# Gathers, first sums and norms at the end of a decoder layer's experts, put in another order

## The chip, the cores and the metric

The kernel runs on one core of one Trainium2 chip. What counts is the time of one execution on the device, in microseconds (us). A core has five engines, each with an instruction queue of its own that it works off in order: TensorE (PE in the profile; PEld is its loading of weights), VectorE (DVE), ScalarE (ACT), GpSimd (POOL) and SyncE (SP), which here only issues transfers. Engines wait for one another through semaphores.

## The reference

One decoder layer over 16 x 256 tokens of 256 values: an attention, a cross attention and a mixture of four experts, each added to the stream and followed by a layer norm without gain. The change touches only the end of the third part:

```python
logits = jnp.einsum('bsh,he->bse', x, router_w) + router_b + load_balancer
rw, sel = jax.lax.top_k(logits, K)           # K = 2 of 4 experts
rw = jax.nn.softmax(rw, axis=-1)
...
gathered = jnp.take_along_axis(stack, sel[..., None], axis=2)
return (rw[..., None] * gathered).sum(axis=2)
...
x = _layernorm(x + _L0_ffn_ref(x, ...), axis=-1)   # (x - m) / sqrt(v + eps)
```

So each token's result is x plus two weighted expert rows, normed over its 256 values.

## The kernel before

The 4096 tokens are 32 rows of 128 (`xs`, one SBUF tile of 128 x 32 x 256 float32) and go in 8 pairs of 4 rows (`CPB` = 4). Pairs 0 to 6 are group 0, pair 7 (`last`) is group 1. While the attention still ran, each token was written by indirect DMA into a list of each expert it chose, one DRAM tensor `xlist[g]` per group; `moe["place"]` holds the token's two places there and `moe["weight"]` its two weights. The place of index 0 is always that of the expert with the lower number.

Each expert works through its list in blocks of 512 rows: `load` fetches a block (SP), `turn` transposes it on TensorE and copies the result with ScalarE and VectorE into a buffer of the ring xeT, the products run, ScalarE applies Gelu, Silu or Relu, and `result` adds the bias on VectorE into the one buffer `ye` and has SP store it over the block's rows in the list. A block of at most 256 rows takes a shorter form; how many rows a list has is known only at run time, so each block stands in `tc.If` branches (`block`, L499 and L502), which every engine passes for itself. The products' PSUM banks are eight, taken in turn (`bank`).

`rest` runs the last stage. Expert 1 of group 0 (`second`) is done first, then experts 2 and 0 together in a loop, then expert 3 (`fourth`) in four blocks, with the three parts of expert 2 of group 1 (`third(1, 0)`, a generator) put between them. `beyond(3, 4, n, fourth)` holds three nested levels for further blocks of expert 3 (L713); with these inputs they are skipped. Then follow experts 0, 1 and 3 of group 1: `first(1, 0)`, `second(1, 0)`, `fourth(1, 0)`.

The results come back by `gather`: four indirect DMAs of GpSimd per pair and choice, from the list into a slot (L671). Slots are the two halves of `ya`, `x3` and, late, the four quarters of a second hidden buffer `hb`. Choice 0 of group 0 needs experts 0 to 2 only, so it is gathered between the blocks of `fourth(0, ..)`, two pairs at a time, and added on VectorE behind each block (`adds`, L682, one instruction per row, `x + t * weight`). Choice 1 of all seven pairs is gathered behind the last of these blocks, 28 transfers in a row. `sums(n)` adds the second choice of n pairs with L682, which also yields each row's sum, and scales these to minus the mean (L691). `end` squares on ScalarE (L701, with a sum per row), takes the inverse root on VectorE (L702, `rsqrt` at L158 to L165, L704), scales the rows on ScalarE (L706) and has SP store each pair (L708). Sums and ends come as 2, 2, 3 and 1 pairs, the first sums ahead of `second(1, 0)`, its end behind it, and so on.

In this stage every engine keeps the order in which the code is written; only in straight code between branches do the engines overlap freely. A gather waits for all earlier stores into its list, and a store into a list for all earlier gathers from it.

Of the kernel before, what the change touches and what calls it, by code (L numbers as in the profile page):

```python
# [20 lines left out]
NPAIR = B // 2  # L21
TB = 2 * S
CPB = TB // P
# [80 lines left out]
def decoder_kernel(ctx: ExitStack, tc: tile.TileContext, a: dict, out: bass.AP):  # L104
    nc = tc.nc
    PE, DVE, ACT, POOL, SP = nc.tensor, nc.vector, nc.scalar, nc.gpsimd, nc.sync
# [3 lines left out]
    out_v = out.flatten_outer_dims().rearrange("(n p) d -> p n d", p=P)  # L110
# [43 lines left out]
    def rsqrt(pool, v, n, E=DVE):  # L154


        yi = pool.tile([P, n], I32, tag=f"rs_y{n}", name="rs_y")
        E.tensor_scalar(yi, v.bitcast(I32), -0.5, float(0x5F3759DF), ALU.mult, ALU.add)  # L158
        y = yi.bitcast(F32)
        t = pool.tile([P, n], F32, tag=f"rs_t{n}", name="rs_t")  # L160
        for _ in range(3):
            if E is DVE:
                E.scalar_tensor_tensor(t, y, -0.5, y, ALU.mult, ALU.mult)  # L163
                E.tensor_tensor(t, t, v, ALU.mult)  # L164
                E.scalar_tensor_tensor(y, t, 1.5, y, ALU.add, ALU.mult)  # L165
# [178 lines left out]
    def group(q):  # L344
        return int(q >= GROUPS[1][0])
# [116 lines left out]
    class Experts:  # L462
# [17 lines left out]
        def next(self, name):  # L480
            t = self.rings[name].pop(0)
            self.rings[name].append(t)
            return t
# [180 lines left out]
            self.loaded += [self.load(0, 2, 0), self.load(0, 0, 0)]  # L664


        def gather(self, q, k):
            t = self.slots.pop(0)
            self.slots.append(t)
            for n in range(CPB):  # L670
                POOL.indirect_dma_start(  # L671
                    t[:, n, :], None, xlist[group(q)][:],
                    bass.IndirectOffsetOnAxis(ap=moe["place"][:, q * CPB + n, k:k + 1], axis=0),
                )
            self.gathered.append((q, k, t))

        def add(self, sums=None):
            q, k, t = self.gathered.pop(0)
            for n in range(CPB):
                x = xs[:, q * CPB + n, :]  # L680
                kw = {} if sums is None else {"accum_out": sums[:, n:n + 1]}
                DVE.scalar_tensor_tensor(  # L682
                    x, t[:, n, :], moe["weight"][:, q * CPB + n, k:k + 1], x, ALU.mult, ALU.add, **kw
                )
            return q, t

        def sums(self, n):

            m = self.fl.tile([P, 3 * CPB], F32, tag="means", name="means", bufs=2)
            done = [self.add(m[:, k * CPB:(k + 1) * CPB]) for k in range(n)]  # L690
            DVE.tensor_scalar(m[:, :n * CPB], m[:, :n * CPB], -1.0 / D, None, ALU.mult)  # L691
            return m, done

        def end(self, m, done):

            w = len(done) * CPB
            m = m[:, :w]
            v = self.fl.tile([P, 3 * CPB], F32, tag="vars", name="vars", bufs=2)[:, :w]
            rows = [(q * CPB + n, t[:, n, :]) for q, t in done for n in range(CPB)]
            for i, (r, t) in enumerate(rows):  # L700
                ACT.activation(t, xs[:, r, :], AF.Square, bias=m[:, i:i + 1], accum_out=v[:, i:i + 1])  # L701
            DVE.tensor_scalar(v, v, 1.0 / D, EPS, ALU.mult, ALU.add)  # L702
            y = rsqrt(self.fl, v, w)
            DVE.tensor_tensor(m, m, y, ALU.mult)  # L704
            for i, (r, t) in enumerate(rows):
                ACT.activation(xs[:, r, :], xs[:, r, :], AF.Identity, bias=m[:, i:i + 1], scale=y[:, i:i + 1])  # L706
            for q, t in done:
                SP.dma_start(out=out_v[:, q * CPB:(q + 1) * CPB, :], in_=xs[:, q * CPB:(q + 1) * CPB, :])  # L708

        def beyond(self, e, i0, i1, work):  # L710

# [8 lines left out]
        def rest(self, fl, xw, xb, rb):  # L720
            self.fl, self.xw, self.xb, self.rb = fl, xw, xb, rb
            self.ring(fl, "hid", 2, [P, 8, TB])
            self.ring(fl, "h2", 1, [P, CPB, D])
            self.ring(fl, "h2T", 1, [P, 2, TB])
            n = SIZES[0] // (4 * P)
            t5 = self.turn(self.loaded.pop(0))
            self.second(0, 4, self.ready.pop(0))
            b_ = self.turn(self.loaded.pop(0))
            self.second(0, 5, t5)
            self.beyond(1, 6, n, self.second)  # L730
            self.known(1)


            ya = self.wb.tile([P, 2, CPB, D], F32, tag="cxp", name="ya")
            self.slots, self.gathered = [ya[:, 0], ya[:, 1]], []
            a_, x0, x1 = self.loaded.pop(0), self.load(0, 3, 0, self.x3), self.load(0, 3, 1, ya[:, 1])
            assert not self.loaded and not self.ready
            with ExitStack() as levels:
                for i in range(n):
                    levels.enter_context(tc.If(self.count[0][4] > 4 * P * i))  # L740
                    a_ = self.turn(a_)
                    b = self.third(0, i, b_)
                    next(b)
                    if i + 1 < n:
                        b_, a1 = self.load(0, 2, i + 1), self.load(0, 0, i + 1)
                    c = self.first(0, i, a_)
                    next(c)
                    next(b)
                    if i + 1 < n:
                        b_, a_ = self.turn(b_), a1  # L750
                    next(c)
                    next(b)

            pairs = iter(range(NPAIR - 1))

            def gathers(k, most=2):
                for _ in range(most):
                    q = next(pairs, None)  # L760
                    if q is not None:
                        self.gather(q, k)

            def adds():
                while self.gathered:
                    self.add()

            x2, y2, x3 = self.load(0, 3, 2), self.load(1, 2, 0), self.load(0, 3, 3)
            ta, tb = self.rings["xeT"]
            self.turn(x0, ta)  # L770
            self.turn(x1, tb)
            gathers(0)
            self.fourth(0, 0, ta)
            adds()
            gathers(0)
            b = self.third(1, 0, self.turn(y2, ta))
            next(b)
            self.turn(x2, ta)
            y0, y1 = self.load(1, 0, 0), self.load(1, 1, 0)
            self.fourth(0, 1, tb)  # L780
            adds()
            gathers(0)
            next(b)
            self.turn(x3, tb)
            y3 = self.load(1, 3, 0)
            self.fourth(0, 2, ta)
            adds()
            gathers(0)
            next(b)
            self.turn(y0, ta)  # L790
            self.fourth(0, 3, tb)
            adds()
            self.rings["xeT"] = [tb]
            self.beyond(3, 4, n, self.fourth)


            ha, hb = self.rings["hid"]
            self.rings["hid"] = [ha]
            hb = hb.rearrange("p f t -> p (f t)").rearrange("p (s c d) -> p s c d", s=4, d=D)
            self.slots += [self.x3] + [hb[:, k] for k in range(4)]  # L800
            last = NPAIR - 1
            pairs = iter(range(last))
            gathers(1, last)
            copies = (DVE.tensor_copy, DVE.tensor_copy)
            c = self.first(1, 0, ta)
            next(c)
            self.turn(y1, tb, copies=copies)
            next(c)
            self.turn(y3, ta, copies=copies)
            part = self.sums(2)  # L810
            self.second(1, 0, tb)
            self.end(*part)
            part = self.sums(2)
            self.gather(last, 0)
            self.fourth(1, 0, ta)
            self.gather(last, 1)
            self.end(*part)
            self.end(*self.sums(3))
            self.add()
            self.end(*self.sums(1))  # L820
            assert not self.gathered

    experts = Experts

# [875 lines left out]
```

## Time and profile before

| | us |
|---|---|
| median of 8 runs | 1749.22 (1746.13 to 1751.86) |
| the profiled execution | 1748.03 |
| its span in the profile | 1746.3 |
| PE busy | 1634.1 (94%) |
| DVE, ACT, POOL busy | 918.2, 969.7, 537.2 |

A line of a timeline or a chain gives the start in us from the span's begin, the time in us, engine, source line, operation and output<-inputs by the program's names, how many, and in brackets how long the engine sat idle before and what ended that. The stages of the end, from the timeline of PE:

| stage | us |
|---|---|
| fourth(0, 0) | from 1515.67 |
| fourth(0, 1) | from 1552.44 |
| fourth(0, 2) | from 1591.62 |
| fourth(0, 3) | from 1626.85 |
| first(1, 0) | from 1656.99 |
| second(1, 0) | from 1681.22 |
| fourth(1, 0) | from 1695.00 |
| last matmul's result read (L546) | 1712.49 |
| last store issued (L708) | 1741.82 |

### The profile page before, as it was taken

The numbers are of one execution on the slowest core, as the hardware profiler recorded it, in microseconds if no ns is written. First come the engines' busy times: TensorE is split into PE (matmuls) and PEld (weight loads), VectorE is DVE, ScalarE is ACT, GpSimd is POOL, SyncE is SP. The second block draws the span as 40 slices with busy tenths as digits, with TensorE's granted clock in tenths as the row PEclk, the third lists the DMA queues.
The fourth block names the chain that finished last, engine by engine and source line by source line (L and its number), as shares of the span: only waits on it lengthen the run. The fifth ranks groups of instructions, "written<-read, shape, count | busy, mean of one in ns | idle before, by whom it ended". The sixth has DMA issues, their size and how long they took to land. (4 is left out here: it accounts for less than half of the span.)

```text
span 1746.3 us, 32316 instructions
## 1 busy us (share of the span) xinstructions
PE 1634.1 (94%) x12254; PEld 959.6 (55%) x12254; DVE 918.2 (53%) x1911; ACT 969.7 (56%) x1463; POOL 537.2 (31%) x1235
## 2 busy tenths in 40 slices
PE   7999999999999899999999999989899999899892
PEld 2344444344444466566666666655566658566671
DVE  2235565556555787777777777674223234222233
ACT  4457667777787856666666666654323221322246
POOL 5000233113133231333554536465411110212061
PEclk9999999999999999999999999998899999999996
DMA  9932112113121300000001000010326011211133
GB/s 252 298 97 68 61 58 73 60 51 98 62 70 65 122 15 2 15 3 15 26 21 33 14 15 24 5 38 26 109 76 209 1 49 50 76 61 49 45 115 115
DMA packets 117771, 115.34 MB, mean 66 GB/s; under 512 B 7776, under 2 KB 111408, under 8 KB 117584
## 3 DMA queue, kind: packets, MB, share of 16 engines
q1 hardware_dynamic: 108560, 93.08, 16.7%
q0 software_dynamic: 7824, 19.65, 3.8%
q8 instruction: 114, 1.87, 0.5%
q14 instruction: 73, 0.60, 0.1%
q10 hardware_dynamic: 1200, 0.15, 0.1%
HBM read 73.79 MB, written 38.54 MB: 64 GB/s over the span
## 5 line engine op out<-in xcount | busy, mean ns | idle before, releaser
L1392 DVE TENSOR_REDUCE mpad<-p 128x4 f32<-128x1024 f32 x256 | 302.1, 1217 | 112.4 <-PE p L152 111.6
L923 ACT ACTIVATE h<-ph,L_attn_b 128x1024 f32<-128x1024 f32 x256 | 271.2, 1110 | 157.2 <-PE ph L152 155.2
L1398 ACT ACTIVATE e<-p 128x512 f32<-128x512 f32 x512 | 268.2, 601 | 131.3 <-PE p L152 130.7
L152 PE MATMUL p<-qp,kT 32*128 32x256 f32 x2048 | 286.6, 399 | 3.1 <-issue 1.4
L152 PE MATMUL p<-kT,qp 32*128 32x256 f32 x2048 | 272.0, 396 | 6.6 <-DVE mpad L1392 6.4
L152 PEld LDWEIGHTS p<-kT,qp 32*128 32x128 f32 x2048 | 192.6, 186 | 47.9 <-DVE mpad L1392 22.5
L152 PEld LDWEIGHTS p<-qp,kT 32*128 32x128 f32 x2048 | 205.8, 188 | 21.3 <-PE p L152 6.7
L152 PE MATMUL ph<-qT,w1p 32*128 32x512 f32 x1024 | 160.2, 643 | 6.1 <-ACT h L923 3.9
L1017 DVE TENSOR_TENSOR z<-rqb,ra 128x1024 f32<-128x1024 f32 x120 | 151.4, 1267 | 3.6 <-DMA rqb<-rqd 3.6
L152 PE MATMUL pe<-h,w2p 128*32 128x512 f32 x1024 | 135.7, 600 | 0.0
L152 PE MATMUL pob<-e,vaug 128*32 128x512 f32 x1024 | 128.6, 621 | 0.0
L1024 ACT ACTIVATE z<-z 128x1024 f32<-128x1024 f32 x120 | 126.5, 1056 | 0.1
L152 PEld LDWEIGHTS ph<-qT,w1p 32*128 32x128 f32 x1024 | 45.3, 183 | 122.8 <-ACT h L923 67.8
L197 POOL TENSOR_SCALAR ln_ve<-ln_mv 128x2 f32<-128x2 f32 x32 | 7.1, 223 | 283.6 <-DVE ln_mv L195 282.9
L671 POOL DMA_INDIRECT ya<-xlist,place x44 | 42.1, 957 | 160.6 <-DVE h2T L519 52.4
L152 PE MATMUL pw<-xeT,L_ffn_sw_w 128*128 128x512 f32 (+1 forms) x256 | 85.0, 494 | 2.4 <-DVEq L713 2.4
L201 POOL TENSOR_SCALAR xs<-xs,ln_mv,rs_y 128x256 f32<-128x256 f32 x64 | 83.0, 1301 | 2.9
L152 PE MATMUL po<-z,vaug 128*32 128x256 f32 x1024 | 74.6, 389 | 6.0 <-ACT z L1024 4.3
L444 POOL DMA_INDIRECT xlist<-xs,place x64 | 63.9, 999 | 50.3 <-DVE place L442 26.6
L152 PEld LDWEIGHTS pw<-xeT,L_ffn_sw_w 128*128 128x128 f32 x256 | 49.8, 195 | 36.3 <-issue 31.5
L1425 ACT COPY ovTb<-pob 128x512 f32<-128x512 f32 x64 | 37.5, 585 | 57.0 <-PE pob L152 57.0
L152 PE MATMUL pr<-L_ffn_ml_w,hid 128*128 128x256 f32 x288 | 64.8, 386 | 1.9 <-ACT hid L586 1.9
(366 smaller groups left out, 2574.4 us busy)
## 6 DMA issues: line engine op xcount, KB each, us to landing
rqb<-rqd SPq DMA_DIRECT2D x64, 512.0 KB
xlist<-zero SPq DMA_DIRECT2D x16, 1024.0 KB
xe<-xlist SPq DMA_DIRECT2D x20, 512.0 KB
xlist<-ye SPq DMA_DIRECT2D x14, 512.0 KB
xs<-in_x SPq DMA_DIRECT2D x8, 512.0 KB
cx<-in_ctx SPq DMA_DIRECT2D x8, 512.0 KB
qp<-st SPq DMA_DIRECT2D x256, 2.0 KB
out<-xs SPq DMA_DIRECT2D x8, 512.0 KB
```

The costliest lines, as they stand in the source:

```text
L152: PE.matmul(out=out_, lhsT=lhsT, rhs=rhs, start=start, stop=stop)
L197: POOL.tensor_scalar(ve, mv[:, :, 1], EPS, None, ALU.add)
L201: POOL.tensor_scalar(x, x, mv[:, i, 0:1], r[:, i:i + 1], ALU.subtract, ALU.mult)
L444: put = POOL.indirect_dma_start(xlist[g][:], bass.IndirectOffsetOnAxis(ap=place[:, n, k:k + 1], axis=0), xs[:, q * CPB + n, :], None)
L671: POOL.indirect_dma_start(t[:, n, :], None, xlist[group(q)][:], bass.IndirectOffsetOnAxis(ap=moe["place"][:, q * CPB + n, k:k + 1], axis=0),)
L923: ACT.activation(h, phs[gp], AF.Tanh, bias=b1[:, fc:fc + 1])
L1017: DVE.tensor_tensor(z, bc(rqbs[u][:, 2 * gp:2 * gp + 2], 2, 2), bc(rk, 3, S), ALU.mult)
L1024: ACT.activation(z, z, AF.Exp)
L1392: DVE.tensor_reduce(mpads[j % 2][:, 2 * gp:2 * gp + 2, :, ic], p1, AX.X, ALU.max, negate=True)
L1398: ACT.activation(e[:, gi], p2[gi], AF.Exp)
L1425: ACT.copy(o, po)
```

## The change

Choice 0 of group 0 is added on GpSimd, in two instructions per pair over 128 x 1024 (`add`), instead of four on VectorE; each pair's `add` and gather stand between the blocks. Choice 1 of pairs 0, 1 and 2 is gathered into `x3` behind `fourth(0, 0)`, `(0, 1)` and `(0, 2)`, the blocks that are sure to hold the pair's rows, and summed, squared and scaled one block later, pair by pair. Pairs 3 and 4 are gathered behind `fourth(0, 3)` and have their sums and squares ahead of `second(1, 0)`; pairs 5 and 6 (with a copy of their places made behind `turn(y3)`) ahead of `fourth(1, 0)`. `sums`, `squares`, `deviations` and `end` are now separate steps. For pair 7 choice 0 is added on GpSimd while `fourth(1, 0)` runs; its squares and scalings are split, two rows on ScalarE and two on VectorE, and it is stored row by row.

```diff
+        def add(self, q, k, t):
+
+            w = moe["weight"][:, q * CPB:(q + 1) * CPB, k]
+            POOL.tensor_tensor(t, t, bc(w, 2, D), ALU.mult)
+            POOL.tensor_tensor(self.rows(q), self.rows(q), t, ALU.add)
+
+        def sums(self, *done):
...
                 DVE.scalar_tensor_tensor(
-                    x, t[:, n, :], moe["weight"][:, q * CPB + n, k:k + 1], x, ALU.mult, ALU.add, **kw
+                    x, t[:, n, :], moe["weight"][:, q * CPB + n, 1:2], x, ALU.mult, ALU.add, accum_out=m[:, i:i + 1]
                 )
...
+        def squares(self, m, rows, vector=()):
+
+            v = self.fl.tile([P, 2 * CPB], F32, tag="vars", name="vars", bufs=3)[:, :len(rows)]
             for i, (r, t) in enumerate(rows):
-                ACT.activation(t, xs[:, r, :], AF.Square, bias=m[:, i:i + 1], accum_out=v[:, i:i + 1])
+                x = xs[:, r, :]
+                if i in vector:
+                    DVE.scalar_tensor_tensor(t, x, m[:, i:i + 1], x, ALU.add, ALU.mult, accum_out=v[:, i:i + 1])
+                else:
+                    ACT.activation(t, x, AF.Square, bias=m[:, i:i + 1], accum_out=v[:, i:i + 1])
+            return m, rows, v
+
+        def deviations(self, m, rows, v):
             DVE.tensor_scalar(v, v, 1.0 / D, EPS, ALU.mult, ALU.add)
-            y = rsqrt(self.fl, v, w)
+            y = rsqrt(self.fl, v, len(rows))
             DVE.tensor_tensor(m, m, y, ALU.mult)
...
+        def end(self, m, rows, y, vector=(), per=CPB):
+
+            for i, (r, _) in enumerate(rows):
+                x = xs[:, r, :]
+                if i in vector:
+                    DVE.tensor_scalar(x, x, y[:, i:i + 1], m[:, i:i + 1], ALU.mult, ALU.add)
+                else:
+                    ACT.activation(x, x, AF.Identity, bias=m[:, i:i + 1], scale=y[:, i:i + 1])
+            for i in range(0, len(rows), per):
+                r = rows[i][0]
+                SP.dma_start(out=out_v[:, r:r + per, :], in_=xs[:, r:r + per, :])
...
-            gathers(0)
+            self.gather(0, 0, s0)
+            self.gather(1, 0, s1)
             self.fourth(0, 0, ta)
-            adds()
-            gathers(0)
+            self.add(0, 0, s0)
+            self.gather(2, 0, s0)
+            self.add(1, 0, s1)
             b = self.third(1, 0, self.turn(y2, ta))
             next(b)
             self.turn(x2, ta)
             y0, y1 = self.load(1, 0, 0), self.load(1, 1, 0)
+            self.gather(0, 1, s2)
+            self.add(2, 0, s0)
+            self.gather(3, 0, s1)
             self.fourth(0, 1, tb)
-            adds()
-            gathers(0)
+            p0 = self.squares(*self.sums((0, s2)))
             next(b)
+            self.add(3, 0, s1)
+            self.gather(4, 0, s0)
             self.turn(x3, tb)
             y3 = self.load(1, 3, 0)
+            p0 = self.deviations(*p0)
+            self.add(4, 0, s0)
+            self.gather(1, 1, s2)
+            self.gather(5, 0, s1)
             self.fourth(0, 2, ta)
-            adds()
-            gathers(0)
+            p1 = self.squares(*self.sums((1, s2)))
             next(b)
+            self.add(5, 0, s1)
+            self.gather(6, 0, s0)
             self.turn(y0, ta)
+            self.end(*p0)
+            p1 = self.deviations(*p1)
+            self.add(6, 0, s0)
+            self.gather(2, 1, s2)
             self.fourth(0, 3, tb)
-            adds()
+            p2 = self.squares(*self.sums((2, s2)))
+            self.end(*p1)
             self.rings["xeT"] = [tb]
             self.beyond(3, 4, n, self.fourth)
...
-            gathers(1, last)
-            copies = (DVE.tensor_copy, DVE.tensor_copy)
+            self.gather(3, 1, s0)
+            self.gather(4, 1, s1)
             c = self.first(1, 0, ta)
             next(c)
+            p2 = self.deviations(*p2)
             self.turn(y1, tb, copies=copies)
             next(c)
             self.turn(y3, ta, copies=copies)
-            part = self.sums(2)
+            self.end(*p2)
+            place = self.fl.tile([P, 2, CPB, 1], I32, tag="place", name="place")
+            DVE.tensor_copy(place, moe["place"][:, 5 * CPB:7 * CPB, 1:2].rearrange("p (q n) k -> p q n k", q=2))
+            p34 = self.squares(*self.sums((3, s0), (4, s1)))
+            p34 = self.deviations(*p34)
+            self.gather(5, 1, hb[:, 0], place[:, 0])
+            self.gather(6, 1, hb[:, 1], place[:, 1])
             self.second(1, 0, tb)
-            self.end(*part)
-            part = self.sums(2)
-            self.gather(last, 0)
+            self.gather(last, 0, hb[:, 2])
+            self.end(*p34)
+            p56 = self.squares(*self.sums((5, hb[:, 0]), (6, hb[:, 1])))
             self.fourth(1, 0, ta)
-            self.gather(last, 1)
-            self.end(*part)
-            self.end(*self.sums(3))
-            self.add()
-            self.end(*self.sums(1))
-            assert not self.gathered
+            self.add(last, 0, hb[:, 2])
+            self.gather(last, 1, hb[:, 3])
+            p56 = self.deviations(*p56)
+            self.end(*p56)
+            half = (2, 3)
+            p7 = self.squares(*self.sums((last, hb[:, 3])), half)
+            self.end(*self.deviations(*p7), half, 1)
```

More of the change, by code (lines that the diff above doesn't have):

```diff
@@ L664, in ahead, with gather @@
             self.loaded += [self.load(0, 2, 0), self.load(0, 0, 0)]
-        def gather(self, q, k):
-            t = self.slots.pop(0)
-            self.slots.append(t)
+        def gather(self, q, k, t, place=None):
+            if place is None:
+                place = moe["place"][:, q * CPB:(q + 1) * CPB, k:k + 1]
             for n in range(CPB):
                 POOL.indirect_dma_start(
-                    t[:, n, :], None, xlist[group(q)][:],
-                    bass.IndirectOffsetOnAxis(ap=moe["place"][:, q * CPB + n, k:k + 1], axis=0),
-                )
-            self.gathered.append((q, k, t))
@@ L677, in add, with rows @@
-        def add(self, sums=None):
-            q, k, t = self.gathered.pop(0)
-            for n in range(CPB):
+                    t[:, n, :], None, xlist[group(q)][:], bass.IndirectOffsetOnAxis(ap=place[:, n, :], axis=0)
+                )
+        def rows(self, q):
+            return xs[:, q * CPB:(q + 1) * CPB, :]
+        def add(self, q, k, t):
+            w = moe["weight"][:, q * CPB:(q + 1) * CPB, k]
+            POOL.tensor_tensor(t, t, bc(w, 2, D), ALU.mult)
+            POOL.tensor_tensor(self.rows(q), self.rows(q), t, ALU.add)
@@ L680, in add @@
+        def sums(self, *done):
+            w = len(done) * CPB
+            m = self.fl.tile([P, 2 * CPB], F32, tag="means", name="means", bufs=3)[:, :w]
+            rows = [(q, n, t) for q, t in done for n in range(CPB)]
+            for i, (q, n, t) in enumerate(rows):
                 x = xs[:, q * CPB + n, :]
-                kw = {} if sums is None else {"accum_out": sums[:, n:n + 1]}
                 DVE.scalar_tensor_tensor(
-                    x, t[:, n, :], moe["weight"][:, q * CPB + n, k:k + 1], x, ALU.mult, ALU.add, **kw
+                    x, t[:, n, :], moe["weight"][:, q * CPB + n, 1:2], x, ALU.mult, ALU.add, accum_out=m[:, i:i + 1]
@@ L684, in add @@
                 )
[L685 to L699, printed above, removed]
-            for i, (r, t) in enumerate(rows):
-                ACT.activation(t, xs[:, r, :], AF.Square, bias=m[:, i:i + 1], accum_out=v[:, i:i + 1])
+            DVE.tensor_scalar(m, m, -1.0 / D, None, ALU.mult)
@@ new lines, in sums @@
+            return m, [(q * CPB + n, t[:, n, :]) for q, n, t in rows]
+        def squares(self, m, rows, vector=()):
+            v = self.fl.tile([P, 2 * CPB], F32, tag="vars", name="vars", bufs=3)[:, :len(rows)]
+            for i, (r, t) in enumerate(rows):
+                x = xs[:, r, :]
[4 more added lines that the diff above has]
+            return m, rows, v
@@ L702, in end @@
+        def deviations(self, m, rows, v):
             DVE.tensor_scalar(v, v, 1.0 / D, EPS, ALU.mult, ALU.add)
-            y = rsqrt(self.fl, v, w)
+            y = rsqrt(self.fl, v, len(rows))
             DVE.tensor_tensor(m, m, y, ALU.mult)
[L705 to L708, printed above, removed]
+            return m, rows, y
@@ L752, in rest @@
                     next(b)
[L756 to L765, printed above, removed]
-                    self.add()
+            s0, s1, s2 = ya[:, 0], ya[:, 1], self.x3
             x2, y2, x3 = self.load(0, 3, 2), self.load(1, 2, 0), self.load(0, 3, 3)
@@ L799, in rest @@
             hb = hb.rearrange("p f t -> p (f t)").rearrange("p (s c d) -> p s c d", s=4, d=D)
-            self.slots += [self.x3] + [hb[:, k] for k in range(4)]
+            copies = (DVE.tensor_copy, DVE.tensor_copy)
             last = NPAIR - 1
-            pairs = iter(range(last))
-            gathers(1, last)
-            copies = (DVE.tensor_copy, DVE.tensor_copy)
+            self.gather(3, 1, s0)
+            self.gather(4, 1, s1)
             c = self.first(1, 0, ta)
             next(c)
+            p2 = self.deviations(*p2)
             self.turn(y1, tb, copies=copies)
@@ L809, in rest @@
             self.turn(y3, ta, copies=copies)
-            part = self.sums(2)
+            self.end(*p2)
[5 more added lines that the diff above has]
+            self.gather(6, 1, hb[:, 1], place[:, 1])
             self.second(1, 0, tb)
-            self.end(*part)
-            part = self.sums(2)
-            self.gather(last, 0)
+            self.gather(last, 0, hb[:, 2])
+            self.end(*p34)
+            p56 = self.squares(*self.sums((5, hb[:, 0]), (6, hb[:, 1])))
             self.fourth(1, 0, ta)
-            self.gather(last, 1)
-            self.end(*part)
-            self.end(*self.sums(3))
-            self.add()
-            self.end(*self.sums(1))
-            assert not self.gathered
+            self.add(last, 0, hb[:, 2])
[5 more added lines that the diff above has]
+            self.end(*self.deviations(*p7), half, 1)
     experts = Experts
```

## The prediction

> **What bounds it now.** I read the slices and the end of the chain first, then each engine's timeline from 1500 us on. Up to 1712 us the end of the kernel is a row of matmul blocks with TensorE nearly always busy. After that nothing but sums, norms, one gather and stores is left, on VectorE and ScalarE by turns. The chain from there:
>
> ```profile
> 1715.59 4.92 DVE xs L682 x24
> 1720.73 6.01 ACT hid L701 x24
> ...
> 1729.80 5.49 ACT xs L706 x11
> 1735.29 1.97 ACT ya L701 x8
> ```
>
> (start, us, what; a summed row counts twice, as its accumulator is read by an instruction of its own.) 12 + 4 rows are summed, squared and scaled after the last matmul, while the last gather was issued long before its turn (GpSimd's and VectorE's timelines):
>
> ```profile
> 1712.49 0.80 DVE L546 TENSOR_TENSOR ye<-pr,L_ffn_ml_b_bc 128x256 f32<-128x256 f32 x2 [10.91 <-PE pr L152]
> 1716.22 0.99 POOL L671 DMA_INDIRECT ya<-xlist,place  x1 [11.84 <-DMA xlist<-ye]
> ```
>
> So two things set the end: when TensorE finishes (call the first L546 there Y, 1712.5), and the tail from Y to the end, 1746.3 - 1712.5 = 33.8 us.
>
> **The tail after the change.** Only pair 7's second half and the scaling of pairs 5 and 6 remain. From Y: store of the block issued at 0.8 (1713.32 in SP's queue), first gather at 3.7, fourth at 7.5, its landing 3.7 later (the median of these four; with 2.8 elsewhere it would be 0.9 sooner): 11.2. The last row's L682, 0.5, and the means, 0.3: 12.0. Squares, two rows on ScalarE (0.5 each and 0.2 for the accumulator) beside two on VectorE (0.41): 13.2. The inverse root, 1737.29 to 1739.72 in the last group now, 2.4: 15.6. Two scalings of 0.5 a side: 16.7. Four stores of 128 KB, 0.4 each on SP, the first after one row: last issued at 17.7. Landing: 512 KB took 2.9 and 256 KB 2.2 (1741.82 to 1744.7, 1713.32 to 1715.5), so about 1.9: 19.6. End work 1.6 as now: **21.2**, a gain of **12.6**. Pairs 5 and 6 don't collide: VectorE 2.4, then 8 rows on ScalarE at 0.5, done at Y + 7.4, ahead of the 12.0.
>
> **What it does to Y.** The new norms stand in the queues of ScalarE and VectorE between the matmul blocks, and an engine runs its queue in order. Block by block, in times of before:
>
> *Behind fourth(0,0)* eight L682 go (3.25 us), so the copy of the turned tokens at 1547.90 no longer holds TensorE: -1.1 of idle, and the half-clock stretch after it (see below) -1.6 at most: **-2.4** (-1.1 to -2.8).
>
> *Behind fourth(0,1)* come 4 sums (1.65), means (0.3), 4 Squares (2.1) ahead of ScalarE's copy of h2T, which was at 1580.41 and will be at 1584.55, done 1584.95. TensorE now runs two matmuls early and goes on at 1584.17; with all 16 behind 1585.0 it ends 1.0 later, with a longer idle: 1.0 + 1.6 = **+2.6**.
>
> *Behind fourth(0,2)* the same, ScalarE's copy from 1620.91 to 1623.8; next block from 1626.85 to about 1628.6: **+1.7**.
>
> *At the skipped levels of L713.* Here is the wait the title doesn't show. An engine that skips them still sets a mark for the work skipped, once its own queue is empty; the first product of first(1,0) takes banks that the skipped work used last and waits for the marks:
>
> ```profile
> 1656.99 15.74 PE L152 MATMUL pw<-xeT,L_ffn_sw_w 128*128 128x256 f32 x64 [2.42 <-DVEq L713]
> L713 ACTq EVENT_SEMAPHORE  x2: 17/17/17, 1329.2 to 1641.5; - x2
> L713 DVEq EVENT_SEMAPHORE  x2: 21/21/21, 1332.3 to 1656.7; - x2
> ```
>
> (TensorE's timeline, and the view of line 713.) VectorE's mark came at 1656.7, when its L682 ended, and TensorE started at 1656.99. ScalarE's came at 1641.5, when its last Gelu ended. Now ScalarE has Squares of pair 2 there (means at 1656.9, plus 2.1) and the scalings of pair 1 (2.1): mark at 1661.2, **+4.4**. If TensorE needed only VectorE's mark it would be +0.3; I take 4.4, since the banks of the skipped Gelus are among those it takes next.
>
> *Ahead of second(1,0)* the sums of pairs 3 and 4 stay at 1682.3, behind the copies of turn(y3), plus 0.25 for the copy of place; but their 8 Squares now run before the Gelus, not after them:
>
> ```profile
> 1683.14 0.69 ACT L555 ACTIVATE hid<-pw,mb 128x512 f32<-128x512 f32 x1 [9.23 <-PE pw L152]
> 1685.66 0.17 DVE L691 TENSOR_SCALAR means<-means 128x8 f32<-128x8 f32 x1
> 1688.09 7.07 PE L152 MATMUL pr<-L_ffn_me_c2w,hid 128*128 128x256 f32 x32
> 1688.99 1.28 ACT L701 ACT_TABLE_LOAD   x1
> ```
>
> Means 1686.0, Squares 4.1, table 1.3, first Gelu 0.7: 1692.1, where the product started at 1688.1: +4.0, and a half-clock stretch 1.6: **+5.6**. The Gelu's four banks are filled meanwhile, so nothing of it is hidden.
>
> *Ahead of fourth(1,0)* ScalarE had 8 scalings and a table, with the product at 1703.97, 8.95 behind the last matmul of second(1,0). Now it has sums of pairs 5, 6 (0.6 after that matmul, 3.6 with means), 8 Squares 4.1, table 1.3, Gelu 0.5: 10.1: **+0.9** with the stretch (now 1.9 us idle, then 3.1).
>
> Sum: -2.4 + 2.6 + 1.7 + 4.4 + 5.6 + 0.9 = **+12.8** on Y, against 12.6 off the tail.
>
> **The half-clock stretch.** After 1.9 us of idle before the product at 1703.97 the granted clock was 0.50 for 3.3 us:
>
> ```profile
> 1582.50:1585.90 3.40, 1.73 (x8) 1.55 (x9) 1.61 (x5) 0.61 (x2) 1.29 (x2) 1.00 0.17 58
> 1585.90:1589.30 3.40, 3.40 (x18) 2.99 (x17) 0.00 (x0) 2.57 (x4) 2.52 (x3) 1.00 0.43 119
> 1702.00:1705.30 3.30, 1.39 (x7) 1.19 (x7) 0.00 (x0) 3.27 (x8) 1.91 (x2) 1.00 0.97 319
> 1705.40:1708.70 3.30, 3.30 (x9) 2.66 (x8) 0.00 (x0) 3.27 (x8) 0.00 (x0) 0.50 0.26 81
> ```
>
> (stretch, length, TensorE busy, ..., clock third from the end.) With 1.39 us busy of a stretch the next one is halved, with 1.73 it isn't. A half stretch costs up to 1.7; with a 4 us stall placed at every position against stretches of 3.4 us and a threshold between those two rows, it averages 1.6, 0.8 at the least and 2.5 at the most. The Trainium skill ("TensorE: Matmul & The Clock Gate", "What's actually happening") has the clock fall only after at least one idle window of about 3.4 us. By that rule the 1.9 us stall would have cost nothing and the new 4 us ones only now and then, and Y would be some 4 us less late; the rows above differ from it and decide.
>
> **Work put at nothing.** GpSimd takes 28 row sums of group 0 as 7 pairs of two instructions over 128x1024. Nearest rows: L891, two inputs of 128x1024, 2.38; L1460, a broadcast second input of 128x512, 1.06, so 2.1: 4.5 a pair, 32 in all, in the gaps between gathers (26, 26 and 31 us idle before L671 now). Followed in its order with 1.26 a gather, the gather for pair 1's sums lands at 1609 and is needed at 1619.8; pair 2's lands at 1644, needed 1655; the gathers that the stores of list 0 must let pass end 5 us ahead of each. Upper end: L201, 1.30 per 128x256, so 10.4 a pair; cover is gone from about 7.3. ScalarE's tables: Square, scaling and copy follow each other without a load now, so only those counted are new, at 1.3, since L701 started at 1690.29 behind its load of 1688.99. The skill's "ScalarE: Activation LUTs" ("What ACT_TABLE_LOAD costs") speaks against Squares between Gelus, with 1.38 us of drain beside the load's 1.28; by it second(1,0) and fourth(1,0) would each be 1.4 later than summed, and the row just named shows no drain. SP gets stores of pairs 0 to 2 between the blocks: pair 1's waits for ScalarE until 1661.2, and SP's marks of L713 stand behind it, so the gathers of pairs 3 and 4 start near 1663, not 1659.6, and land at 1676, needed at 1682.
>
> **Rivals.** *A, the norms hide:* TensorE doesn't wait for ScalarE's mark (-4.1), and the stalls behind fourth(0,1) and ahead of second(1,0) cost no clock (-3.2): Y +5.5 against -12.6, about 1742. For it: VectorE's mark is the only one that the profile shows being waited for. Against: ScalarE's was merely early, and the order ahead of second(1,0) is plain. *B, slower, the clock:* each of the four stalls that are now 4 us or longer (two copies, the mark, second(1,0)) falls across two stretches and pays 2.5 for 1.6, +3.6, and the first block gains only 1.1, +1.3: about 1754; it decides from 0.9 a stall. For it: three of the four stalls of 1.9 to 2.7 us now paid the full 1.7; against: their positions in the stretches are chance. *C, slower, GpSimd becomes the bound:* at L201's 10.4 the gather for pair 1 lands 4 us late and that for pair 2 10 us, both straight onto TensorE: 1763; it decides from 7.3 a pair. Against: L628 holds 0.72 throughout.
>
> **Numbers.** The profiled run took 1748.03 with a span of 1746.3, 1.2 below the median of 1749.22. Span 1746.3 + 12.8 - 12.6 = 1746.5, so 0.2 over the median: **1749.4**. The forecast's own range, with the clock at 0.8 to 2.5 a stall, the first block 1.4 and the tail 1 either way: 1745 to 1753. A measurement tells 0.2% (3.5 us) from nothing. No change 0.42; A 0.28; B 0.20; C 0.10. So faster 0.28, same 0.42, slower 0.30. The range reaches to near A and B: 1741 to 1756.
>
> **What would show it.** Right: ScalarE's mark at L713 some 4 us after the block's result, and TensorE's first L571 product just behind it; about 4 us of idle before the product of second(1,0) with half clock after; tail near 21 us from the last L546. Wrong: TensorE starting while ScalarE still scales pair 1; a gather landing after VectorE asks for it; GpSimd's 128x1024 over 3.6 us each.

## The result, and the profile after

The changed kernel takes **1758.62 us** in the median of 11 runs (1753.91 to 1759.83), against 1748.85 of the kernel before in the same comparison: a ratio of 1.0053, 95% interval 1.0043 to 1.0062. It is slower by 9.8 us, where 1749.4 and "no change" were forecast, with 1741 to 1756 as the range.

The profiled execution has a span of 1756.0 us. Cut into the stages of the forecast, each from the first product of a block to that of the next (the last one from the first L546 of fourth(1, 0) to the end of the span):

| stage from | before | after | difference | forecast |
|---|---|---|---|---|
| fourth(0, 0) | 36.77 | 33.78 | -3.0 | -2.4 |
| fourth(0, 1) | 39.18 | 48.03 | **+8.9** | +2.6 |
| fourth(0, 2) | 35.23 | 39.33 | **+4.1** | +1.7 |
| fourth(0, 3), with the skipped levels | 30.14 | 35.55 | +5.4 | +4.4 |
| first(1, 0) | 24.23 | 25.28 | +1.1 | 0 |
| second(1, 0) | 13.78 | 19.45 | +5.7 | +5.6 |
| fourth(1, 0) to L546 | 17.49 | 16.87 | -0.6 | +0.9 |
| the tail | 33.81 | 20.71 | -13.1 | -12.6 |
| sum | 230.63 | 239.00 | +8.4 | +0.2 |

So the tail came down as forecast, and the sum went wrong by what TensorE loses ahead of it. Its waits, in its timeline of the changed kernel (start, us, engine, line, operation, output<-inputs, in brackets the idle time before and what ended it):

```profile
1588.07 6.57 PE L152 MATMUL pw<-h2T,L_ffn_ce_f1w 128*128 128x256 f32 x16 [9.15 <-ACT h2T L519]
1632.86 3.78 PE L152 MATMUL pr<-L_ffn_ce_gen_w,h2T 128*128 128x256 f32 x8 [5.91 <-ACT h2T L519]
1673.69 16.79 PE L152 MATMUL pw<-xeT,L_ffn_sw_w 128*128 128x256 f32 x64 [7.78 <-ACTq L731]
1709.72 8.86 PE L152 MATMUL pr<-L_ffn_me_c2w,hid 128*128 128x256 f32 x32 [3.71 <-ACT hid L555]
1728.45 7.17 PE L152 MATMUL pr<-L_ffn_ml_w,hid 128*128 128x256 f32 x32 [2.97 <-ACT hid L586]
```

Every one of them is now ended by ScalarE, and at the skipped levels (L713 before, L731 now) by the mark that ScalarE sets behind its queue. The longest wait is the one that the forecast had at 4.4 us (the copy done at 1584.95, the transposes at 1580.59). VectorE, GpSimd and ScalarE in that stretch:

```profile
1578.95 0.72 POOL L628 TENSOR_TENSOR h<-h,L_ffn_ce_n1g_bc 128x256 f32<-128x256 f32 x1 [5.93 <-issue]
1579.34 0.62 DVE L693 SCALAR_TENSOR_TENSOR xs<-x,weight,xs 128x256 f32<-128x256 f32 x1 [0.39 <-issue]
1579.89 0.93 DVE L693 SCALAR_TENSOR_TENSOR xs<-x,weight,xs 128x256 f32<-128x256 f32 x1
1580.50 0.90 POOL L628 TENSOR_TENSOR h<-h,L_ffn_ce_n1g_bc 128x256 f32<-128x256 f32 x1
1580.75 0.93 DVE L693 SCALAR_TENSOR_TENSOR xs<-x,weight,xs 128x256 f32<-128x256 f32 x1
...
1582.23 2.07 POOL L683 TENSOR_TENSOR ya<-ya,weight 128x1024 f32<-128x1024 f32 x1
1582.59 1.74 DVE L696 TENSOR_SCALAR means<-means 128x4 f32<-128x4 f32 x1
1584.39 1.28 ACT L707 ACT_TABLE_LOAD   x1 [18.99 <-DVE means L696]
1585.69 0.51 ACT L707 ACTIVATE x<-xs,means 128x256 f32<-128x256 f32 x1
...
1587.67 0.35 ACT L519 COPY h2T<-pt 128x256 f32<-128x256 f32 x1
```

Three things are to be read here. A row's sum takes up to 0.93 us, where it takes 0.48 (0.41 from one to the next) behind fourth(0, 2). The means over 128x4, 0.17 us elsewhere, take 1.74 and end at 1584.33, just behind GpSimd's L683, which ends at 1584.30. And ScalarE, idle for 18.99 us, loads its table only when the means are there, so the 1.28 us lie in the open. Rows, means and load are 1.6, 1.4 and 1.3 over the forecast, 4.3 of the 4.75 by which the idle time exceeds it.

The tail answers to the forecast closely: the block's store was issued 0.8 behind the first L546, the four gathers began 3.7 behind it, and the means were done at 11.9, for 12.0 summed. From the same timeline:

```profile
1735.29 0.80 DVE L546 TENSOR_TENSOR ye<-pr,L_ffn_ml_b_bc 128x256 f32<-128x256 f32 x2 [12.80 <-PE pr L152]
1739.00 0.99 POOL L673 DMA_INDIRECT hid<-xlist,place  x1 [5.15 <-DMA xlist<-ye]
1747.02 0.17 DVE L696 TENSOR_SCALAR means<-means 128x4 f32<-128x4 f32 x1
```

### The profile page after: what moved, and what is told of

It is laid out like the page before. It is cut to its first block, busy times and chain, and to the rows that moved or that the text cites. A ratio compares the mean times of both kernels' runs of the same rounds, so it can differ in the third digit from the quotient of the medians.

```text
span 1756.0 us, 32274 instructions
## 1 busy us (share of the span) xinstructions
PE 1636.4 (93%) x12254; PEld 961.7 (55%) x12254; DVE 921.3 (52%) x1912; ACT 967.4 (55%) x1457; POOL 571.9 (33%) x1251
## 5 line engine op out<-in xcount | busy, mean ns | idle before, releaser
L673 POOL DMA_INDIRECT ya<-xlist,place x36 | 34.6, 960 | 97.4 <-DMA xlist<-ye 35.9
```

The source lines that it names most:

```text
L673: POOL.indirect_dma_start(t[:, n, :], None, xlist[group(q)][:], bass.IndirectOffsetOnAxis(ap=place[:, n, :], axis=0))
```

## The experiments

Ten runs follow, two of them of the two kernels again. These two, the table loaded ahead and the version with all moves together ran on one chip. The other six ran on two further chips; there, what lies ahead of fourth(0, 0) was 6 to 12 us longer than in the profiles above, and the kernel before took 1785 and 1783 us, for a reason that no profile shows (its mean granted clock was 0.959 to 0.964 in these runs, 0.968 to 0.975 on the first chip). All six variants were faster than it there, with ratios of 0.973 to 0.986. The changed kernel itself wasn't run on those chips, so whether it is slower than the kernel before there stays open. These ratios are not used; the six are compared by stages and by the sum from fourth(0, 0) to the end, 239.0 us for the changed kernel (230.6 for the kernel before).

### Squares of pairs 0 and 1 late

```diff
-            p0 = self.squares(*self.sums((0, s2)))
+            p0 = self.sums((0, s2))
             next(b)
...
-            p0 = self.deviations(*p0)
+            p0 = self.deviations(*self.squares(*p0))
             self.add(4, 0, s0)
```

and the same for pair 1.

> The Squares of pairs 0 and 1 move from between VectorE's sums and ScalarE's copy of h2T to ahead of fourth(0,2) and fourth(0,3); the sums stay. Stages are counted between the first products of successive blocks. Theory (ScalarE's Squares, with a table load that waits for the means, hold the copy of h2T): the copy comes some 0.5 us behind the transposes again, and TensorE waits only for VectorE's half, about 3.5 us as its four sums are still slow beside GpSimd; fourth(0,1) to fourth(0,2) goes from 48.0 to about 41.5 us, fourth(0,2) to fourth(0,3) from 39.3 to about 34 us; total about 12 us less, near 1747 us. Rival (VectorE's sums and its half of the copy bind, the Squares only lie beside them): the first stage stays above 46 us and the total falls by less than 4 us.

Measured: the two stages 44.23 and 32.85 us, the sum from fourth(0, 0) 228.8, so 10.3 less. The second stage is 1.1 us shorter than expected, and shorter than in the kernel before (now four rows, not eight, stand ahead of VectorE's copy). The first lies between the two theories: ScalarE's copy is early again, but VectorE's half is later than reckoned. GpSimd's L683 and VectorE's and TensorE's rows:

```profile
1592.92 2.07 POOL L683 TENSOR_TENSOR ya<-ya,weight 128x1024 f32<-128x1024 f32 x1
1593.29 1.74 DVE L696 TENSOR_SCALAR means<-means 128x4 f32<-128x4 f32 x1
1594.94 0.41 DVE L519 COPY h2T<-pt 128x256 f32<-128x256 f32 x1
1595.40 6.13 PE L152 MATMUL pw<-h2T,L_ffn_ce_f1w 128*128 128x256 f32 x14 [4.85 <-DVE h2T L519]
```

4.85 us of idle, and then 14 matmuls in 6.13 us, which took 3.29 before: 2.8 us of the stage are slow clock.

### The operations on h2 on VectorE

```diff
-                    POOL.tensor_tensor(h2[:, c, :], h2[:, c, :], fw["ce_n1g"], ALU.mult)
-                    POOL.tensor_tensor(h2[:, c, :], h2[:, c, :], self.rb, ALU.add)
+                    DVE.tensor_tensor(h2[:, c, :], h2[:, c, :], fw["ce_n1g"], ALU.mult)
+                    DVE.tensor_tensor(h2[:, c, :], h2[:, c, :], self.rb, ALU.add)
```

> Only the two operations on h2 at L628 and L629 move from GpSimd to VectorE, behind both copies of h2T; the sums of pair 0 then have no GpSimd arithmetic beside them, or only the end of a pair's addition. Theory (VectorE's sums are slow because GpSimd computes at the same time, 0.93 for 0.41 us a row, and the means 1.74 for 0.17 us): rows 0.41 us, means 0.17 us, TensorE's idle time ahead of the first product of the feed-forward falls from 9.15 to about 6 us, the stage from 48.0 to about 44.8 us, total 3 us less. Rival (the sums are slow by their own operands, just gathered rows or the first use of that slot): rows stay near 0.9 us, the stage near 48 us, the total the same. The table load of 1.28 us ahead of the Squares stays in both.

Measured: idle 6.54 us, stage 44.47, sum 234.2. The theory holds row by row. GpSimd now has only the end of a pair's addition beside the sums:

```profile
1583.03 2.35 POOL L684 TENSOR_TENSOR xs<-xs,ya 128x1024 f32<-128x1024 f32 x1
1584.71 0.95 DVE L693 SCALAR_TENSOR_TENSOR xs<-x,weight,xs 128x256 f32<-128x256 f32 x1 [0.38 <-issue]
1585.60 0.48 DVE L693 SCALAR_TENSOR_TENSOR xs<-x,weight,xs 128x256 f32<-128x256 f32 x1
...
1586.93 0.17 DVE L696 TENSOR_SCALAR means<-means 128x4 f32<-128x4 f32 x1
1587.16 1.28 ACT L707 ACT_TABLE_LOAD   x1 [16.39 <-DMA xlist<-ye]
```

The one row that overlaps L684 (until 1585.38) is the one that is long; the next, and the means, are at their usual time. The rows' own operands are no cause.

### Both together

The edits are the two just shown.

> The first two experiments together: Squares of pairs 0 and 1 late, and L628 and L629 on VectorE. Each alone left the stage from fourth(0,1) to fourth(0,2) at 44.2 and 44.5 us of 48.0. Theory (without the Squares TensorE waits for VectorE's half of the copy, which GpSimd's arithmetic makes late): rows of the sums 0.41 us and at most one longer, the means 0.17 us, idle time ahead of the remaining 14 matmuls from 4.85 to about 2.2 us, stage 39 to 41.5 us by where the clock falls; the next stage near 32.9 us. Rival (the rest of e1's stage has another cause than GpSimd, such as the order of VectorE's queue alone): idle time stays above 4 us and the stage above 43 us.

Measured: 3.15 us idle, 41.18 us for the stage, then 32.52; sum 224.3. The means are at 0.17 and one row at 1.23, beside L684. Idle time is 0.95 over the expected 2.2. That row alone is 0.75 over its usual 0.48, and between the means and the copy lies a gap of 0.55, which the run before it has too and the changed kernel hasn't; its cause is open. So of the 8.9 us of this stage, the Squares and GpSimd's neighbourhood together hold 6.9; of the remaining 2.0, 0.5 is idle time and 1.5 clock (14 matmuls in 4.77 us for 3.29).

### Work behind the skipped levels

```diff
-            p2 = self.squares(*self.sums((2, s2)))
-            self.end(*p1)
+            p2 = self.sums((2, s2))
             self.rings["xeT"] = [tb]
...
             next(c)
-            p2 = self.deviations(*p2)
+            p2 = self.squares(*p2)
+            self.end(*p1)
             self.turn(y1, tb, copies=copies)
             next(c)
+            p2 = self.deviations(*p2)
             self.turn(y3, ta, copies=copies)
```

> The Squares of pair 2 and the scaling of pair 1 move from ahead of the skipped levels to behind the first half of first(1,0); the sums of pair 2 stay. Theory (TensorE's first product of first(1,0) waits for ScalarE's mark, which stands behind them): it starts about 0.3 us after VectorE's mark, the stage from fourth(0,3) to first(1,0) goes from 35.6 to about 30 us, the next stages change by less than 1 us, total about 5 us less. Rival (TensorE waits for VectorE's mark, or for something else there): the stage stays above 34 us. Second rival (the wait only moves): the 5 us come back ahead of second(1,0), whose copies and Gelus then stand behind the Squares.

Measured: the stage goes from 35.55 to 30.70 us, and TensorE waits for VectorE's mark:

```profile
1678.75 0.17 DVE L696 TENSOR_SCALAR means<-means 128x4 f32<-128x4 f32 x1
1679.58 15.74 PE L152 MATMUL pw<-xeT,L_ffn_sw_w 128*128 128x256 f32 x64 [2.94 <-DVEq L731]
```

The mark is shown to be the cause. Half of the gain moved on, though, as the second rival had it: second(1, 0) to fourth(1, 0) grew from 19.45 to 21.86 us, because the inverse root of pair 2 (1703.48 to 1705.80 on VectorE) then stands ahead of the copies of turn(y3) and the sums of pairs 3 and 4 come later; sum 235.3.

### Squares of pairs 3 and 4 behind second(1, 0)

```diff
-            p34 = self.squares(*self.sums((3, s0), (4, s1)))
-            p34 = self.deviations(*p34)
+            p34 = self.sums((3, s0), (4, s1))
...
             self.gather(last, 0, hb[:, 2])
-            self.end(*p34)
-            p56 = self.squares(*self.sums((5, hb[:, 0]), (6, hb[:, 1])))
+            p34 = self.deviations(*self.squares(*p34))
+            p56 = self.sums((5, hb[:, 0]), (6, hb[:, 1]))
             self.fourth(1, 0, ta)
+            self.end(*p34)
+            p56 = self.squares(*p56)
```

> The Squares of pairs 3 and 4 move behind second(1,0) and their scaling, with the Squares of pairs 5 and 6, behind the Gelus of fourth(1,0); all sums stay. Theory (the Squares hold the Gelus of second(1,0), TensorE waits and runs at half clock after): the stage from second(1,0) to fourth(1,0) goes from 19.5 to about 14 us, from there to the first L546 from 16.9 to 16 to 18 us, the tail stays near 21 us; total about 5 us less. Rival (the gain is given back at the end, since ScalarE then has 16 rows and two table loads to do during the product of fourth(1,0)): the tail grows by over 3 us and the total falls by less than 2 us.

Measured: 13.78 us from second(1, 0), as before the change, 13.63 from fourth(1, 0) instead of 16.87, a tail of 20.97; sum 230.3, so 8.7 less. More than expected, since the Gelus of fourth(1, 0) lose their wait as well. TensorE no longer waits at all here, and ScalarE does the moved rows during the last product:

```profile
1711.89 7.07 PE L152 MATMUL pr<-L_ffn_me_c2w,hid 128*128 128x256 f32 x32
1725.70 7.07 PE L152 MATMUL pr<-L_ffn_ml_w,hid 128*128 128x256 f32 x32
...
1727.75 4.04 ACT L723 ACTIVATE xs<-xs,means,rs_y 128x256 f32<-128x256 f32 x8
```

### The two kernels again, and the table loaded ahead

> The kernel before, unchanged, for a second profile of it on one chip with the others of this call: the runs of it beside the first four experiments were 1785 us, against 1748 us beside the changed kernel, and no profile shows where the 36 us lie. If they lie ahead of the change's first place, all kernels of one chip carry them and stage times decide; the stages from fourth(0,1) on should be 39.2, 35.2, 30.1, 24.2, 13.8 and 17.5 us and the tail 33.8 us, as in the first profile. If they lie in these stages, the earlier comparison of stages falls.

Measured: 1749.81 us (10 runs), ratio to before 1.0005, interval 0.9991 to 1.0018. The stages are the same as in the first profile within 0.1 us, but for two: 37.04 us from fourth(0, 0), not 36.77, and 41.66 us from fourth(0, 1), not 39.18, with the same wait of 2.63 us ahead of the 14 matmuls, which then took 4.89 instead of 3.29 (the block's first product took 14.77 instead of 13.90). Against this profile the changed kernel lost 6.3 us in that stage on the same chip, not 8.9. What a wait costs by the clock is thus not fixed even for one program.

> The changed kernel, unchanged, on the same chip as the kernel before and the two versions of this call. Stages from fourth(0,1) on again 48.0, 39.3, 35.6, 25.3, 19.5 and 16.9 us, tail 20.7 us, each within 0.3 us; together 9 to 10 us more than before. A ratio to before under 1.000 would say that what lies ahead of these stages moved the times of one program against the other by more than the change itself.

Measured: 1758.2 us (6 runs), ratio 1.005, interval 1.0032 to 1.0067; stages 47.93, 39.33, 35.50, 25.26, 19.45 and 16.87, tail 20.70.

```diff
+            ACT.activation(self.fl.tile([P, 1], F32, tag="warm", name="warm"), ident[:, :1], AF.Square)
             p0 = self.squares(*self.sums((0, s2)))
```

and the same ahead of pairs 1 and 2.

> The changed kernel with one Square over 128x1 ahead of the sums of pairs 0, 1 and 2, which depends on nothing recent, so that ScalarE loads its table before it waits for the means. Theory (the load stands behind the wait and is paid in full, three times): the three stages from fourth(0,1) to first(1,0) shrink by 1.3 us each, to about 46.7, 38.0 and 34.3 us, total 3.9 us less. Rival (the load is hidden beside VectorE's half of the copy or the wait for other marks): no stage changes by over 0.3 us.

Measured: 1754.83 us (10 runs), 3.4 below the changed kernel on the same chip; stages 45.54, 38.06 and 34.29. ScalarE's first row and the wait of the first of them:

```profile
1582.72 1.74 DVE L696 TENSOR_SCALAR means<-means 128x4 f32<-128x4 f32 x1
1584.54 0.51 ACT L707 ACTIVATE x<-xs,means 128x256 f32<-128x256 f32 x1 [17.50 <-POOL ya L683]
1586.93 5.36 PE L152 MATMUL pw<-h2T,L_ffn_ce_f1w 128*128 128x256 f32 x16 [7.87 <-ACT h2T L519]
1703.79 10.10 PE L152 MATMUL pr<-L_ffn_me_c2w,hid 128*128 128x256 f32 x32 [3.72 <-ACT hid L555]
```

The Squares start 0.08 behind the means, and idle time falls by 1.28: the load was paid in full. Two of the three stages are 1.2 to 1.3 us shorter, the first 2.5, as the clock fell less there. Part of it went again: the product of second(1, 0), behind the same wait of 3.7 us, took 10.10 us instead of 8.86.

### All moves together

```diff
-            p0 = self.squares(*self.sums((0, s2)))
             next(b)
             self.add(3, 0, s1)
             self.gather(4, 0, s0)
             self.turn(x3, tb)
             y3 = self.load(1, 3, 0)
-            p0 = self.deviations(*p0)
+            p0 = self.deviations(*self.squares(*self.sums((0, s2))))
```

the same for pair 1; for pair 2 and the scaling of pair 1 as in the experiment on the skipped levels, with the sums of pair 2 moved too; and the experiment on pairs 3 to 6.

> All four causes together: sums and Squares of pairs 0 and 1 go ahead of fourth(0,2) and fourth(0,3), behind the turned tokens; those of pair 2 and the scaling of pair 1 behind the first half of first(1,0); the Squares of pairs 3 and 4 behind second(1,0); the scaling of these and the Squares of pairs 5 and 6 behind fourth(1,0). Theory (the change lost only by where its norms stand in the queues; gathers, GpSimd's sums and the tail are as they were): stages about 36.5, 32, 29, 24.2, 13.8 and 14 us, tail 21 us, so about 25 us less than the kernel before, ratio 0.985. Rival (sums later make the gathers that reuse their slot late, and TensorE waits for VectorE again): some stage stays within 1 us of the changed kernel's and the ratio is above 0.992.

Measured: **1724.59 us** (5 runs, 1723.75 to 1727.15), ratio to before 0.9862, interval 0.9843 to 0.988, 24.7 us below the kernel before and 33.6 below the changed one on the same chip. Stages 36.66, 33.67, 29.62, 24.23, 13.78 and 13.64, tail 20.81: the second is off by 1.7, the third by 0.6. The gathers are in time. VectorE and GpSimd still meet, now in the middle of a block, and it isn't free: the Squares wait for the means, the Gelus stand behind the Squares, and TensorE waits 0.53 us for the Gelus, in the stage that is off most:

```profile
1591.80 2.05 POOL L683 TENSOR_TENSOR ya<-ya,weight 128x1024 f32<-128x1024 f32 x1 [1.93 <-DMA ya<-xlist,place]
1592.03 2.10 DVE L693 SCALAR_TENSOR_TENSOR xs<-x,weight,xs 128x256 f32<-128x256 f32 x1
1593.93 2.41 POOL L684 TENSOR_TENSOR xs<-xs,ya 128x1024 f32<-128x1024 f32 x1
1594.17 2.19 DVE L696 TENSOR_SCALAR means<-means 128x4 f32<-128x4 f32 x1
...
1596.45 0.51 ACT L707 ACTIVATE x<-xs,means 128x256 f32<-128x256 f32 x1 [9.95 <-DVE means L696]
...
1599.84 4.73 ACT L586 ACTIVATE hid<-pw,L_ffn_ml_b 128x512 f32<-128x512 f32 x8
1600.58 14.52 PE L152 MATMUL pr<-L_ffn_ml_w,hid 128*128 128x256 f32 x64 [0.53 <-ACT hid L586]
```

One row of 0.48 us takes 2.10, the means take 2.19; each ends just behind GpSimd's instruction, at 1594.13 against 1593.85 and 1596.36 against 1596.34.

```diff
-            POOL.tensor_tensor(t, t, bc(w, 2, D), ALU.mult)
-            POOL.tensor_tensor(self.rows(q), self.rows(q), t, ALU.add)
+            for n in range(CPB):
+                x = xs[:, q * CPB + n, :]
+                DVE.scalar_tensor_tensor(
+                    x, t[:, n, :], moe["weight"][:, q * CPB + n, k:k + 1], x, ALU.mult, ALU.add
+                )
```

> The version with the norms in the slack, with the first sums (L683 and L684) back on VectorE, one fused operation for each row, at the same places in the program. Theory (GpSimd's sums are hidden and what they hold up on VectorE is now hidden too, so they are worth what VectorE's rows would hold): the stage from fourth(0,0) grows by 2 to 3 us, as eight rows again stand ahead of the copies behind it, the others change by less than 1 us, the tail by less than 1 us, total 2 to 4 us above the 1724.6 us of that version. Rival (the shared access costs more than GpSimd's help is worth): total the same or lower.

Measured, against the version just shown: 36.35 us from fourth(0, 0) (+2.6), 1.2 less from fourth(0, 2), where TensorE's wait of 0.53 is gone, 1.1 more from fourth(1, 0); the sum 208.1 against 206.1. GpSimd's sums are worth some 2 us net, at the low end of what was expected: they save 2.6 behind fourth(0, 0) and give part of it back behind fourth(0, 2), where what they hold up on VectorE isn't hidden, though it was expected to be.

## Why the prediction was wrong

**Right.** The tail: 20.7 us for 21.2. Behind fourth(0, 0): -3.0 for -2.4. The skipped levels: TensorE waited for ScalarE's mark, and taking the Squares and scalings from ahead of it gave 4.9 us back. Ahead of second(1, 0): +5.7 for +5.6, and with the Squares moved the stage was 13.78 again. GpSimd's pair of sums: 1.91 + 2.35 = 4.26 us for the 4.5 taken; no gather came late enough to hold TensorE. But Y came 21.5 us later, not 12.8 (1735.29 for 1712.49, with 1.3 us of the difference ahead of fourth(0, 0)).

**The step that failed** is "Behind fourth(0,1)": "come 4 sums (1.65), means (0.3), 4 Squares (2.1) ahead of ScalarE's copy of h2T ... +2.6". It measured +8.9: 6.3 of the 8.2 us by which the whole sum missed are there. (Between the second profiles it is +6.3; there the kernel before had itself lost 2.5 us to the clock.) The order was right, the durations weren't: they came from rows that ran with GpSimd silent. In the kernel before:

```profile
1580.53 3.24 DVE L682 SCALAR_TENSOR_TENSOR xs<-ya,weight,xs 128x256 f32<-128x256 f32 x8
1584.17 3.29 PE L152 MATMUL pw<-h2T,L_ffn_ce_f1w 128*128 128x256 f32 x14 [2.63 <-DVE h2T L519]
1584.30 0.95 POOL L671 DMA_INDIRECT ya<-xlist,place  x1 [26.02 <-DVE h2T L519]
1594.07 0.74 POOL L628 TENSOR_TENSOR h<-h,L_ffn_ce_n1g_bc 128x256 f32<-128x256 f32 x1
```

The change had taken GpSimd's wait away. Before, its gathers stood ahead of L628 and waited for VectorE's sums, so that L628 and L629 came at 1594.07, long after them; now that queue is free, and L628, L629 and L683 fall on just these sums. Of the miss of 6.3 us, 4.75 are idle time (the rows 1.6, the means 1.4, the load 1.3) and 1.0 is clock (2.6 for the 1.6 put down). The 1.0 summed for the later start was a little low too: 16 matmuls of this shape reach the next product 3.46 us after their start, so it was 1.2 by the rows of before. I followed GpSimd's order for when its gathers land and not for what its arithmetic does to VectorE. One row of the trace of before did show it, far from here: L390 took 0.66 us beside GpSimd's L1460, its like L391, behind it, 0.21.

```profile
1141.99 1.06 POOL L1460 TENSOR_TENSOR ob<-ob,rs_y 128x512 f32<-128x512 f32 x1
1142.47 0.66 DVE L390 TENSOR_TENSOR gt<-lg 128x64 f32<-128x64 f32 x1
```

The Trainium skill has the rule, in "SBUF — State Buffer", "Who interferes with whom": VectorE's instructions with two inputs in SBUF, and those in a mode that takes both ports, contend with GpSimd for one shared pair of ports, and the later one waits until the other is done. The rows above agree as to the waiting, 1.74 for 0.17 and 2.10 for 0.48 us; that it is for ports, no run here shows.

**A second step failed with it:** "ScalarE's tables: Square, scaling and copy follow each other without a load now, so only those counted are new". Behind a Gelu, Square needs a load, and it isn't made while ScalarE waits for the means but after: 1.3 us in each of three stages, which the run with the load ahead showed. It makes half of the miss of 2.4 behind fourth(0, 2), whose other half was not taken apart, and more than all of the 1.0 at the mark.

**The clock** was taken at 1.6 a stall. It cost 2.6 behind fourth(0, 1) (16 matmuls in 6.57 us, where 2 and 14 took 0.70 and 3.29 before) and, with nothing put down for it, 1.05 at first(1, 0) (16.79 for 15.74); at fourth(1, 0) it was less than before: the product took 7.17 us, not 8.86. Rival A fell with ScalarE's mark. Rival B had the side right (1754, for 1758.6 measured), but the clock alone isn't it: its stalls were to be of 4 us, and those that decided were 9.15, 5.91 and 7.78. Rival C had the engine right and the mechanism wrong: GpSimd was fast enough, and cost by its neighbourhood.

What stays open: why the kernel before took 1783 to 1785 us on the other chips, while the variants of the changed one were at 1736 to 1762; and the gap of 0.55 us ahead of VectorE's copy.

## What to carry to other kernels

When work leaves a queue or a wait is removed from it, look at what then runs at the same time as what, not only at when it ends: VectorE's duration is only good for a sum if GpSimd was doing the same beside it. Put norms and other small work in an engine's queue behind the instructions that the matmul engine waits for, at a place where that engine has much work ahead of it: from fourth(0, 0) to the last L546 the two orders of the same work took 218.3 and 185.3 us. A table load counts as exposed where the first instruction that needs it waits for data, as it did in three stages here, and a tiny instruction ahead of the wait hid it.

## What the runs showed of the hardware

VectorE's instruction beside GpSimd's, in the rows above, doesn't slow down in proportion but waits for its end: over 128x4 elements 1.74 and 2.19 us for 0.17, each ending 0.02 to 0.03 us behind GpSimd's; rows of 128x256 ended 0.28 behind it. GpSimd loses too, though less (L628 0.90 for 0.72). Not every instruction is held: a copy of turned tokens out of PSUM (L519, 128x512) at 1638.38 in the changed kernel took 0.69 us wholly beside GpSimd's L683 (1637.66 to 1639.56), and two such copies in a row took 1.29 with GpSimd's arithmetic silent.

What an idle stretch costs by the clock depends on how it falls: the same product behind the same wait of 3.7 us took 8.86 and 10.10 us in two kernels, 7.07 without a wait. In the profile of the changed kernel around the longest wait (stretch, length, busy time of PE, PEld, DVE, ACT and POOL, granted clock, DMA share, GB/s):

```profile
1582.30:1585.70 3.40, 0.00 (x0) 0.00 (x0) 2.31 (x4) 1.30 (x2) 3.32 (x2) 0.70 0.00 0
1585.70:1589.10 3.40, 1.03 (x3) 0.85 (x4) 0.00 (x0) 2.32 (x9) 2.95 (x3) 0.50 0.14 37
1589.10:1592.50 3.40, 3.40 (x9) 2.68 (x8) 0.00 (x0) 0.95 (x2) 1.92 (x3) 0.50 0.33 93
1592.50:1595.90 3.40, 3.40 (x14) 2.90 (x13) 0.00 (x0) 0.95 (x2) 2.26 (x2) 0.80 0.09 29
```

The clock fell while TensorE was idle and stayed at half through a stretch in which it was busy throughout: a long wait here is paid once as idle time and again in the matmuls behind it.
